# A four-stage graph network: head 3's attention weights turned by transfers, first questions by node chunk, bias rows added by transfers, terms dealt anew

## The chip, the cores and the metric

The kernel runs on one core of one Trainium2 chip. The metric is device time in microseconds, the median of several executions. TensorE does the matrix products, VectorE and ScalarE the elementwise work, and transfers are issued from the queues of SyncE (SP) and GpSimd (POOL).

## The reference, cut to what matters

512 nodes with 512 features pass through four residual stages. The first is a graph convolution. The second is a transformer of four blocks with four heads each, whose attention runs over the edges. The third is a diffusion over the graph. The fourth is a relational convolution of two layers, whose weights are sums over 30 basis matrices for each of two relations. The parts that the change touches, by their algebra:

```python
# second stage, block i; src, dst: 16384 edges among 512 nodes
y = cond_layer_norm(x, cond, s1, b1)
q = (y @ wq + bq) * 128 ** -0.5          # 4 heads of 128
k = y @ wk + bk
v = y @ wv + bv
scores = sum(q[src] * k[dst])            # per edge and head
attn = softmax of scores over the edges of each src
x = x + (segment_sum(attn * v[dst], src) @ wo + bo)
y = cond_layer_norm(x, cond, s2, b2)
x = x + relu(y @ m_w1 + m_b1) @ m_w2 + m_b2
# fourth stage, layer l
w = einsum('rb,bio->rio', att_l, basis_l)   # 2 relations, 30 bases of 512 x 512
msg = sigmoid(x_j @ gate_w[r]) * x_j @ w[r] # r by edge type
out = segment_sum(msg, row) + x @ root + bias
```

## The kernel before

The 512 nodes lie in four chunks of 128 partitions (K = 4), and so do the features. Everything is float32 except parts of the graph's counts. The edges are first turned into dense matrices of counts between nodes. Attention is therefore dense: the scores of a head are a 512 x 512 product, to which `lnC` (the logarithm of the number of edges, very negative where there is none) is added.

The order of instructions on each engine is the order in which the program writes them (`tc.manual_schedule()`), and each engine takes its queue in that order. No planner decides anything. Tiles come from pools: a tile under a name that is in use waits until the old one's readers are done. `one` has one buffer for each name, so `v`, `oT`, `mod` and `yT` are each taken in turn by several things. `weights` has four buffers of 1 MB, `rows` two, `turned` and `pT` two each, `bases` three. In PSUM, `mm` (name `ps`) has two banks, `tr` two and `sp` four.

One block `i` goes as follows.

- The first normalisation leaves `yT`, chunk by chunk. Behind each chunk's transposes (`norm_T`) TensorE computes the values of that chunk (`v_part(c)`, L832). That covers the wait for the next chunk.
- Three projections follow (`q_of`, `k_of`, L943), and then head after head: `weigh_head` computes four score chunks (L959), VectorE adds `lnC` and finds the minimum (L963), ScalarE takes the exponential (L965), VectorE the reciprocal (L952), and ScalarE scales the weights (L955).
- The product with the values (`gather`) wants the weights transposed. For heads 0 to 2, `turn_by_blocks` transposes 32 x 32 blocks on VectorE (L978), and 16 transfers from SyncE's queue put the blocks in their places (L983). For head 3, `turn` uses 16 transposes on TensorE (L121) and copies on ScalarE (L122).
- `rows_of` multiplies by `wo`, the result is added to `z` (L1077), and `norm_chunk` normalises it again under a new `mod` (`modulation`, L702 and L704).
- The MLP's first product is taken in two halves of the nodes (`m1`, L1087). The second is added to `z` (L1117) and normalised for the next block.
- The rows `bo` and `m_b2` are added to all of `z` by four VectorE instructions each (`add_row`, L992).

Beside this, VectorE computes the weights of the fourth stage. `relation_weights` is a generator: each step adds one basis times a scalar to `wrel` (L218), and is called a term below. `more(n)` puts the next n terms into VectorE's queue at that place, so where each `more` stands decides what waits behind terms. A basis is loaded from POOL's queue (L202), two ahead. There are 120 terms, and two empty steps after the last of layer 0, while `wrel` of that layer is written out to `w1d` (L220) to make room for layer 1.

The tail has the second MLP product into `x` (L1160), the diffusion (L1167, L1177, L1179) and the two relational layers.

Of the kernel before, what the change touches and what calls it, by code (L numbers as in the profile page):

```python
# [19 lines left out]
P = 128  # L20
# [47 lines left out]
def network(ctx, tc, a, out, flag_i, general):  # L68
# [17 lines left out]
    def by_partition(v):  # L86
        return v.rearrange("(k p) o -> p k o", p=P)

    def load_w(src):
        w = weights.tile([P, K, D], F32, name="w")  # L90
        nc.sync.dma_start(w, by_partition(src))
        return w
# [105 lines left out]
    def relation_weights():  # L198

        def load(l, b):  # L200
            t = pools["bases"].tile([P, K * D], F32, name="basis")
            nc.gpsimd.dma_start(t.rearrange("p (k o) -> p k o", k=K), by_partition(a[f"L3_gnn_basis{l + 1}"][b]))  # L202
            return t

        todo = [(l, b) for l in range(2) for b in range(BASES)]
        ahead = [load(*todo[i]) for i in range(2)]
        for i, (l, b) in enumerate(todo):
            if b == 0:
                wrel.append([pools["w"].tile([P, K * D], F32, name=f"wrel{r}") for r in range(R)])
            if i + 2 < len(todo):  # L210
                ahead.append(load(*todo[i + 2]))
            t = ahead[i]
            for r in range(R):
                s, w = att[:, l, r * BASES + b : r * BASES + b + 1], wrel[l][r]
                if b == 0:
                    nc.vector.tensor_scalar(w, t, s, None, op0=OP.mult)
                else:
                    nc.vector.scalar_tensor_tensor(w, t, s, w, op0=OP.mult, op1=OP.add)  # L218
                if l == 0 and b == BASES - 1:
                    nc.gpsimd.dma_start(w1d[:, r, :], w)  # L220
                yield
            if l == 0 and b == BASES - 1:

                yield
                yield

# [14 lines left out]

    def load_block(i, names):
        return [load_w(a["L1_gnn_" + n][i]) for n in names]

# [473 lines left out]
    nc.sync.dma_start(C1d, C01[:, 1, :, :])  # L718
    wv, wq, wk = load_block(0, ("wv", "wq", "wk"))

# [103 lines left out]
    def enter_d(c):  # L824
        n = rsqrt_end(*inner[c])
        nc.vector.scalar_tensor_tensor(ys[c], ys[c], n, mod[:, 1, c, :], op0=OP.mult, op1=OP.add)

    def v_part(c):
        if general:
            nc.vector.tensor_tensor(v[:, c, :], nodes(yT, c, wv), bv_row, op=OP.add)  # L830
        else:
            nc.scalar.copy(v[:, c, :], nodes(yT, c, wv))  # L832
# [63 lines left out]
    s_start(1)  # L896
    v = one.tile([P, K, D], F32, name="v")
    v_part(0)
    enter_b(2)
# [7 lines left out]
    enter_d(2)  # L907
    v_part(1)
    enter_b(3)
# [6 lines left out]
    if not general:  # L916
# [3 lines left out]
        nc.vector.tensor_scalar(flag_i, ps[:1, :1], 0.5, None, op0=OP.is_gt)  # L920
    v_part(2)
    enter_d(3)
# [15 lines left out]
    with ExitStack() as ph:  # L938
# [6 lines left out]

        def weigh_head(qT, kT):

            ps_, done = [], []

            def finish_chunk():  # L950
                c, p, st = done.pop(0)
                nc.vector.reciprocal(st[:, 2:3], st[:, 1:2])  # L952
                if general:
                    nc.vector.tensor_mul(st[:, 2:3], st[:, 2:3], has[:, c : c + 1])
                nc.scalar.mul(p, p, st[:, 2:3])  # L955

            for c in range(K):
# [7 lines left out]
                nc.scalar.activation(p, ns, AF.Exp, bias=st[:, 0:1], scale=-1.0, accum_out=st[:, 1:2])  # L965
                ps_.append(p)
                done.append((c, p, st))
                if c:
                    finish_chunk()
            finish_chunk()  # L970
            return ps_

        def turn_by_blocks(ps_):


            t = att_p.tile([P, 4, K, K, 32], F32, name="turned", bufs=2)
            for c in range(K):
                nc.vector.transpose(t[:, :, :, c, :].rearrange("p b k i -> p k b i"),  # L978
                                    ps_[c].rearrange("p (k b i) -> p k b i", k=K, b=4))
            pT = att_p.tile([P, 4, K, P], F32, name="pT", bufs=2)  # L980
            for a in range(4):
                for b in range(4):
                    nc.sync.dma_start(pT[32 * b : 32 * b + 32, a, :, :], t[32 * a : 32 * a + 32, b, :, :, :])  # L983
            return pT

        def turn(pT, ps_, cs):
            for c in cs:
                transposed(pT[:, :, chunk(c)], [ps_[c][:, chunk(k)] for k in range(K)], nc.scalar.copy)

        def add_row(row):  # L990
            for c in range(K):
                nc.vector.tensor_tensor(z[:, c, :], z[:, c, :], row, op=OP.add)  # L992

        for i in range(NB):
            oT = one.tile([P, H, N], F32, name="oT")
            turned = []

            def gather(j):


                pT, o, bias = turned[j], oT[:, j, :], bv[:, i, j : j + 1]
                bank = dict(pool=sp, name="sp") if j > 1 else {}
                if j < H - 1:
                    ps = product([(v[:, k, chunk(j)], pT[:, :, k, :]) for k in range(K)], **bank)
                    ps = ps.rearrange("p (a c i) -> p a c i", a=4, c=K)
                    o = o.rearrange("p (c a i) -> p a c i", c=K, a=4)
                else:
                    ps = product([(v[:, k, chunk(j)], pT[:, k, :]) for k in range(K)], **bank)
                if general:
                    nc.vector.tensor_copy(o, ps)  # L1010
                else:
                    nc.scalar.activation(o, ps, AF.Identity, bias=bias)

# [6 lines left out]

            q, k = [q_of(0)], [k_of(0)]
            q.append(q_of(1))
            for j in range(H):
                head = weigh_head(q[j], k[j])
                if j < H - 1:
                    turned.append(turn_by_blocks(head))
                if j == 0:
                    k.append(k_of(1))
                    q.append(q_of(2))
                    more(1)  # L1030
                elif j == 1:
                    k.append(k_of(2))
                    v_part(3)
                    more(2)
                elif j == 2:
                    gather(0)
                    mod = new_mod()
                    modulation(mod, 0)
                    q.append(q_of(3))
                    k.append(k_of(3))  # L1040
                    gather(1)
                    add_row(bo)
                    more(3)
            w1, w2 = load_block(i, ("m_w1", "m_w2"))
            b2 = load_row(a["L1_gnn_m_b2"][i])

# [7 lines left out]

            ps_ = [rows_of(c, (0, 1)) for c in range(2)]
            more(6)
            pT = att_p.tile([P, K, N], F32, name="pT", bufs=2)
            turn(pT, head, range(K))
            turned.append(pT)
            modulation(mod, 1)  # L1060
            if i < NB - 1:
                modulation_loads(i + 1, 1)
            if i == 0 and not general:
                missed = nc.values_load(flag_i[:1, :1], min_val=0, max_val=1)
            gather(3)
            gather(2)
            yT = one.tile([P, K, N], F32, name="yT")
            ys = []
            for c in range(K):
                if c < 2:  # L1070
                    ps = rows_of(c, (3, 2), ps_[c], last=True)
                else:
                    ps = rows_of(c, (0, 1))
                    if c == 3:
                        norm_T(yT, ys[1], 1)
                    rows_of(c, (2, 3), ps, last=True)
                nc.vector.tensor_tensor(z[:, c, :], ps, z[:, c, :], op=OP.add)  # L1077
                ys.append(norm_chunk(mod, c))
                if c == 2:
                    norm_T(yT, ys[0], 0)  # L1080
            tT = one.tile([P, K, N], F32, name="oT")

# [13 lines left out]
            m1(0, 3)  # L1096
            add_row(b2)
            if i == NB - 1:
                for c in range(K):
                    nc.vector.tensor_tensor(x[:, c, :], z[:, c, :], x[:, c, :], op=OP.add)  # L1100
            else:
                wv, wq, wk, wo = load_block(i + 1, ("wv", "wq", "wk", "wo"))
                if general:
# [17 lines left out]
            norm_T(yT, ys[1], 1)  # L1121
            v = one.tile([P, K, D], F32, name="v")
            v_part(0)
            more(1)
            norm_T(yT, ys[2], 2)
            v_part(1)
            more(1)
            norm_T(yT, ys[3], 3)
            v_part(2)
            more(7)  # L1130
# [35 lines left out]
    for c in range(K):  # L1166
# [4 lines left out]
        if c:  # L1171
            more(1)
    hT = one.tile([P, K, N], F32, name="yT")
# [136 lines left out]
```

## Time and profile before

| | |
|---|---|
| time, median of 3 runs (lowest to highest) | 833.35 us (833.02 to 836.57) |
| the profiled execution: its own time | 833.25 us |
| its span | 831.5 us |
| TensorE busy (PE) | 807.9 us, 97% |
| VectorE busy (DVE) | 678.5 us, 82% |
| ScalarE busy (ACT) | 325.2 us, 39% |
| terms (L218), 116 of them | 264.9 us on VectorE, 2343 ns each |
| granted TensorE clock | 0.999 |

The span is the time from the first to the last instruction that was profiled. The execution's own time is 1.75 us longer. In a timeline a line gives the start in the span, the duration, the engine and line of the code, what is written and read, and how many instructions were merged; in brackets stands the idle time before it and what ended that. Records of f32 matrix products come in pairs, two for a call. Busy time of TensorE is no measure of its work, since the end of each product is modelled and products overlap.

### The profile page before, as it was taken

The page shows a single profiled execution, that of the slowest core. Times are in us where ns is not written, and L with a number is a line of the kernel's source. Part 1 is how long each engine was busy: PE and PEld are TensorE (multiplying, and loading weights), DVE is VectorE, ACT ScalarE, POOL GpSimd, SP SyncE. Part 2 cuts the span into 40 slices and gives each one's busy share as a digit, 9 for nine tenths or more (in the row PEclk, how much of TensorE's full clock was granted, in tenths as well). Part 3 has the DMA queues.
Part 4 walks back from the last instruction along what each step waited for, and adds up shares of the span by engine and source line. Part 5 has one row for each costly group of instructions (what it writes and reads, how often), then busy time and mean ns, then how long its engine had stood idle before and what let it go on. Part 6 is the DMA issues. An engine that isn't in the chain of part 4 may idle for free.

```text
span 831.5 us, 8251 instructions
## 1 busy us (share of the span) xinstructions
PE 807.9 (97%) x2597; PEld 392.6 (47%) x2597; DVE 678.5 (82%) x1199; ACT 325.2 (39%) x657; POOL 64.4 (8%) x135
## 2 busy tenths in 40 slices
PE   7999999999999999999999999999999999999997
PEld 4444344454444644445644445544445544444445
DVE  5977986978899999799997889998899977787530
ACT  5454414544662424652324652325653122310410
POOL 8000010000000101010101010110010100010000
PEclk9999999999999999999999999999999999999999
DMA  9200164305677646588547585655599721231001
GB/s 228 75 7 17 43 221 184 114 1 165 187 233 253 207 139 202 149 256 276 177 153 269 149 268 201 203 177 172 147 310 362 227 71 53 76 103 50 1 13 40
DMA packets 50833, 128.38 MB, mean 154 GB/s; under 512 B 7008, under 2 KB 7808, under 8 KB 49760
## 3 DMA queue, kind: packets, MB, share of 16 engines
q0 software_dynamic: 17552, 66.83, 25.5%
q1 hardware_dynamic: 32944, 60.84, 23.2%
q8 instruction: 22, 0.36, 0.2%
q14 instruction: 27, 0.22, 0.1%
q10 hardware_dynamic: 288, 0.13, 0.1%
HBM read 108.90 MB, written 6.29 MB: 139 GB/s over the span
## 4 chain that ended last, share of the span: by engine, by line
PE 56%; DVE 27%; ACT 6%; issue 4%; SPq 4%; DMA 2%; DVEq 0%; ACTq 0%
PE ps L101 28%; DVE wrel L218 13%; PE sp L101 6%; PE ps L1087 5%; PE win L598 5%; PE ps L376 5%; SPq L983 3%; ACT p L965 2%; PE sp L959 2%; DVE st L158 2%; PE tr L121 2%; DVE turned L978 2%; PE sp L702 1%; DMA pT<-turned 1%; DVE z L992 1%
## 5 line engine op out<-in xcount | busy, mean ns | idle before, releaser
L218 DVE SCALAR_TENSOR_TENSOR wrel<-basis,att,wrel 128x2048 f32<-128x2048 f32 x116 | 264.9, 2343 | 0.0
L101 PE MATMUL ps<-w,oT 128*128 128x512 f32 (+1 forms) x296 | 129.7, 584 | 1.0 <-DVE x L1160 1.0
L101 PE MATMUL ps<-yT,w 128*128 128x512 f32 x256 | 112.9, 594 | 0.0
L101 PE MATMUL ps<-w,yT 128*128 128x512 f32 x224 | 101.1, 595 | 1.2 <-ACT yT L128 0.7
L202 POOL DMA_DIRECT2D basis<-in_L_gnn_basis_dram x60 | 45.1, 752 | 676.0 <-DVE wrel L218 517.1
L101 PEld LDWEIGHTS ps<-w,oT 128*128 128x128 f32 x296 | 54.6, 190 | 63.9 <-issue 55.2
L101 PEld LDWEIGHTS ps<-yT,w 128*128 128x128 f32 x256 | 48.2, 190 | 61.9 <-issue 61.2
L101 PEld LDWEIGHTS ps<-w,yT 128*128 128x128 f32 x224 | 41.1, 190 | 47.7 <-issue 44.7
L1087 PE MATMUL ps<-yT,w 128*128 128x256 f32 x256 | 58.5, 382 | 2.9 <-ACT yT L122 2.9
L133 ACT ACTIVATE g<-mv,eps_t 128x1 f32<-128x1 f32 (+1 forms) x45 | 13.2, 294 | 121.2 <-DVE mv L160 120.1
L965 ACT ACTIVATE p<-ns,stat 128x512 f32<-128x512 f32 x64 | 45.5, 711 | 31.1 <-DVE stat L963 30.9
L959 PE MATMUL sp<-kT,qT 128*128 128x512 f32 x128 | 57.5, 592 | 0.0
L1087 PEld LDWEIGHTS ps<-yT,w 128*128 128x128 f32 x256 | 47.4, 190 | 14.3 <-ACT yT L122 6.2
L598 PE MATMUL win<-s_hot,st 128*128 128x512 bf16 x195 | 51.2, 381 | 0.0
L963 DVE CUSTOM_DVE_ANT_0 ns<-sp,lnC 128x512 f32<-128x512 f32 x64 | 43.2, 689 | 5.5 <-PE sp L959 5.5
L579 DVE TENSOR_SCALAR s_hot<-node_ids,e_c 128x512 bf16<-128x512 f16 x128 | 39.6, 355 | 6.1 <-PE win L598 5.9
L955 ACT ACTIVATE p<-p,stat 128x512 f32<-128x512 f32 x64 | 43.7, 706 | 0.0
L959 PEld LDWEIGHTS sp<-kT,qT 128*128 128x128 f32 x128 | 24.3, 190 | 30.6 <-issue 30.1
L704 ACT ACTIVATE mod<-sp 128x512 f32<-128x512 f32 x64 | 32.9, 599 | 8.6 <-PE sp L702 8.6
L598 PEld LDWEIGHTS <-st 128*128 128x128 bf16 x195 | 18.6, 98 | 37.3 <-issue 24.1
L952 DVE RECIPROCAL stat<-stat 128x1 f32<-128x1 f32 x64 | 10.4, 163 | 29.8 <-ACT p L965 29.6
L121 PEld LDWEIGHTS tr<-ident,y 128*128 128x128 f32 x176 | 21.5, 141 | 20.7 <-issue 19.4
(273 smaller groups left out, 1097.7 us busy)
## 6 DMA issues: line engine op xcount, KB each, us to landing
basis<-in_L_gnn_basis_dram POOLq DMA_DIRECT2D x60, 1024.0 KB, 6.8
pT<-turned SPq DMA_DIRECT2D x192, 64.0 KB
w<-in_L_gnn_m_w_dram SPq DMA_DIRECT2D x8, 1024.0 KB
w<-in_L_gnn_wv_dram SPq DMA_DIRECT2D x4, 1024.0 KB
w<-in_L_gnn_wq_dram SPq DMA_DIRECT2D x4, 1024.0 KB
w<-in_L_gnn_wk_dram SPq DMA_DIRECT2D x4, 1024.0 KB
w<-in_L_gnn_wo_dram SPq DMA_DIRECT2D x4, 1024.0 KB
w1d<-wrel POOLq DMA_DIRECT2D x2, 1024.0 KB, 6.2
```

The costliest lines, as they stand in the source:

```text
L101: nc.tensor.matmul(ps, lhsT, rhs, start=(first and i == 0), stop=(last and i == len(parts) - 1))
L121: nc.tensor.transpose(ps[:, i, :], b, ident)
L202: nc.gpsimd.dma_start(t.rearrange("p (k o) -> p k o", k=K), by_partition(a[f"L3_gnn_basis{l + 1}"][b]))
L218: nc.vector.scalar_tensor_tensor(w, t, s, w, op0=OP.mult, op1=OP.add)
L376: nc.tensor.matmul(bank[0], lhsT, rhs, start=(i == 0), stop=(i == len(parts) - 1))
L579: nc.vector.tensor_scalar(s, node_ids, src[:, c : c + 1], None, op0=OP.is_equal)
L598: nc.tensor.matmul(banks[w], st[:, c - g0, :, :], s, start=(left[w] == total[w]), stop=(left[w] == 1))
L955: nc.scalar.mul(p, p, st[:, 2:3])
L959: nc.tensor.matmul(ps, qT[:, chunk(c)], kT, start=True, stop=True)
L963: nc.vector.tensor_tensor_reduce(ns, ps, lnC[:, c, :], -1.0, 3e38, OP.add, OP.min, st[:, 0:1])
L965: nc.scalar.activation(p, ns, AF.Exp, bias=st[:, 0:1], scale=-1.0, accum_out=st[:, 1:2])
L1087: nc.tensor.matmul(ps[:, :256], w1[:, k, chunk(j)], yT[:, k, cols], start=(k == 0), stop=(k == K - 1))
```

## The change

- All heads are turned by blocks. `weigh_head` now transposes the blocks itself, chunk 0 ahead of the last chunk's reciprocal. `bring` issues the 16 transfers. Heads 0 and 1 are brought into a `mod` tile that is free at that time, heads 2 and 3 into `pT`.
- The questions and keys of heads 0 and 1 are computed by node chunk behind `norm_T` (`qk_part`, 128 columns a call), where the values were computed. The values follow during heads 2 and 3 and behind them. `qk` and `v` share a buffer.
- The rows `bo` and `m_b2` are added by accumulating transfers from POOL's queue. In the last block `m_b2` is added to `x` at the block's start.
- Terms: none between the heads, 11 after head 3, 6 and 9 later in the block; in the diffusion two in place of one behind each chunk. At the meeting of the layers the last two bases of layer 0 and the first two of layer 1 are taken relation by relation, and the two empty steps are gone. A basis is loaded when one has been used up, three at the start.
- Weights are loaded in the order wq, wk, wv, wo.
- In the second normalisation, chunk 2's `norm_chunk` is written behind the transposes of chunk 1.

```diff
@@ relation_weights
-        ahead = [load(*todo[i]) for i in range(2)]
+        order = [(l, b, r) for l in range(2) for b in range(BASES) for r in range(R)]
+        meet = slice(2 * BASES - 4, 2 * BASES + 4)
+        order[meet] = [(l, b, r) for l, bs in ((0, (BASES - 2, BASES - 1)), (1, (0, 1))) for r in (1, 0) for b in bs]
+        bases = {i: load(*i) for i in todo[:3]}
...
+            used[l, b] += 1
+            if used[l, b] == R and len(bases) < len(todo):
+                i = todo[len(bases)]
+                bases[i] = load(*i)
+            yield
...
+    def qk_part(i, c):
+        ps = mm.tile([P, D], F32, name="ps")
+        for n, (w, j) in enumerate(((wk, 0), (wq, 0), (wk, 1), (wq, 1))):
+            calls(ps[:, chunk(n)], [(w[:, k, chunk(j)], yT[:, k, chunk(c)]) for k in range(K)])
+        for n, b in enumerate((bk, bq, bk, bq)):
+            nc.scalar.activation(qk[:, n, chunk(c)], ps[:, chunk(n)], AF.Identity,
+                                 bias=b[:, i, n // 2 : n // 2 + 1], scale=qscale if n % 2 else 1.0)
...
@@ weigh_head
+            t = att_p.tile([P, 4, K, K, 32], F32, name="turned", bufs=2)
...
+            turn_blocks(0)
             finish_chunk()
-            return ps_
+            for c in range(1, K):
+                turn_blocks(c)
+            if j < 2:
+                if j == 0:
+                    spare.append(new_mod())
+                pT = spare[0][:, j, :, :].rearrange("p a (k n) -> p a k n", k=K)
+            else:
+                pT = att_p.tile([P, 4, K, P], F32, name="pT", bufs=2)
+            return t, pT
...
-        def turn(pT, ps_, cs):
-            for c in cs:
-                transposed(pT[:, :, chunk(c)], [ps_[c][:, chunk(k)] for k in range(K)], nc.scalar.copy)
-        def add_row(row):
-            for c in range(K):
-                nc.vector.tensor_tensor(z[:, c, :], z[:, c, :], row, op=OP.add)
+        def add_row(t, row):
+            nc.gpsimd.dma_start(t, row.unsqueeze(1).to_broadcast([P, K, D]), accum_op=OP.add)
...
@@ a block
-            q, k = [q_of(0)], [k_of(0)]
-            q.append(q_of(1))
+            add_row(z, bo)
+            if i == NB - 1:
+                add_row(x, load_row(a["L1_gnn_m_b2"][i]))
+            qk_part(i, 3)
+            k, q = [qk[:, 0, :], qk[:, 2, :]], [qk[:, 1, :], qk[:, 3, :]]
+            q.append(q_of(2))
             for j in range(H):
-                head = weigh_head(q[j], k[j])
...
+                weighed = weigh_head(j, q[j], k[j])
+                if j == 2:
+                    v = one.tile([P, K, D], F32, name="v")
+                    v_part(0)
+                elif j == 3:
+                    v_part(1)
+                turned.append(bring(*weighed))
                 if j == 0:
-                    k.append(k_of(1))
-                    q.append(q_of(2))
-                    more(1)
+                    k.append(k_of(2))
                 elif j == 1:
...
+            v_part(2)
+            v_part(3)
...
-            ps_ = [rows_of(c, (0, 1)) for c in range(2)]
-            more(6)
-            pT = att_p.tile([P, K, N], F32, name="pT", bufs=2)
-            turn(pT, head, range(K))
-            turned.append(pT)
+            more(11)
+            gather(0)
+            gather(1)
+            mod = new_mod()
+            modulation(mod, 0)
+            ps_ = [rows_of(0, (0, 1))]
             modulation(mod, 1)
+            ps_.append(rows_of(1, (0, 1)))
...
+            gather(2)
             gather(3)
-            gather(2)
...
-            add_row(b2)
...
+                add_row(z, b2)
...
@@ next block's first chunks
-            v = one.tile([P, K, D], F32, name="v")
-            v_part(0)
+            qk = one.tile([P, 4, N], F32, name="v")
+            qk_part(i + 1, 0)
             more(1)
...
@@ diffusion
         if c:
-            more(1)
+            more(2)
```

## The prediction

> **What bounds the kernel now.** I read the page's engine totals, then one attention block (block 1) queue by queue in the timelines, then the tail. All times are microseconds from the start of the span.
>
> ```profile
> span 831.5 us, 8251 instructions
> PE 807.9 (97%) x2597; PEld 392.6 (47%) x2597; DVE 678.5 (82%) x1199; ACT 325.2 (39%) x657; POOL 64.4 (8%) x135
> ```
>
> TensorE looks like the bound, but its timeline shows few holes and VectorE's shows almost none either. VectorE in block 1, from the score minimum of head 0 (call it D) to the first `z` addition behind the attention (call it Z):
>
> ```profile
> 302.35 20.44 DVE L218 SCALAR_TENSOR_TENSOR wrel<-basis,att,wrel 128x2048 f32<-128x2048 f32 x9
> 322.72 0.68 DVE L963 CUSTOM_DVE_ANT_0 ns<-sp,lnC 128x512 f32<-128x512 f32 x1
> ...
> 330.34 2.31 DVE L218 SCALAR_TENSOR_TENSOR wrel<-basis,att,wrel 128x2048 f32<-128x2048 f32 x1
> 332.57 0.68 DVE L963 CUSTOM_DVE_ANT_0 ns<-sp,lnC 128x512 f32<-128x512 f32 x1
> ...
> 337.79 2.49 DVE L978 STREAM_TRANSPOSE turned<-p 128x512 f32<-128x512 f32 x4
> 340.20 4.57 DVE L218 SCALAR_TENSOR_TENSOR wrel<-basis,att,wrel 128x2048 f32<-128x2048 f32 x2
> ...
> 352.40 2.46 DVE L992 TENSOR_TENSOR z<-z,row 128x512 f32<-128x512 f32 x4
> 354.77 6.87 DVE L218 SCALAR_TENSOR_TENSOR wrel<-basis,att,wrel 128x2048 f32<-128x2048 f32 x3
> ...
> 366.55 13.64 DVE L218 SCALAR_TENSOR_TENSOR wrel<-basis,att,wrel 128x2048 f32<-128x2048 f32 x6
> 380.13 0.69 DVE L1077 TENSOR_TENSOR z<-ps,z 128x512 f32<-128x512 f32 x1
> ```
>
> VectorE has no long wait between 322.72 and 380.13: four heads, four row additions, twelve terms, end to end. TensorE has its output rows for the 380.13 addition ready at about 379.9. So both engines bound the block at once, and work taken from one alone buys nothing. TensorE around the turn of head 3 and the start of the MLP:
>
> ```profile
> 366.46 1.04 PE L121 MATMUL tr<-ident,p 128*128 128x128 f32 x8
> 368.19 1.14 PE L121 MATMUL tr<-ident,p 128*128 128x128 f32 x8 [0.69 <-ACT pT L122]
> ...
> 390.45 1.99 PE L1087 MATMUL ps<-yT,w 128*128 128x256 f32 x8 [0.72 <-ACT yT L122]
> ```
>
> The third queue is SyncE's:
>
> ```profile
> 330.45 32.10 SPq L983 DMA_DIRECT2D pT<-turned  x48
> ```
>
> Forty-eight transfers in 32.1, 0.63 to 0.64 each where no wait shows, 10.1 a head. It has no room to spare once a fourth head is added.
>
> **The change, part by part.**
>
> *Head 3 by blocks.* Removed per block: 16 transposes, 0.109 each start to start (four in 0.435), 1.7, and the hole of 0.69. Added: four block transposes on VectorE (2.49 for four) and 16 transfers on SyncE (10.1).
>
> *Questions by chunk.* q0, k0, q1, k1 become 64 calls of 128 columns. The trace has such calls once:
>
> ```profile
> 185.95 1.06 PE L101 MATMUL sp<-CP,AT 128*128 128x128 f32 x8
> ```
>
> Eight records (two a call), next start 0.89 later: 0.111 a record against 0.43 for 512 columns, so a chunk costs 32 x 0.111 = 3.55 against 3.44: +0.1, and 1.8 over 16 chunks. The Trainium skill speaks against the edit here: "TensorE: Matmul & The Clock Gate", section Back-to-back issue gap, puts a sustained stream of weight load and 128-column matmul at about 81 ns instead of the isolated 56. A bf16 call of 512 columns takes 0.216 here, so an f32 record is two passes and the row is 56 ns a pass; at 81 the chunk would cost 5.2, and 16 of them +28. I take the row; it is the same form, though only eight records long.
> ScalarE gets four 128-column evacuations a chunk, about 0.36 each (extrapolated from 0.47 for 256 columns and 0.69 for 512), under 3.5 of matmuls.
> The values move behind the scores, where TensorE used to have questions and keys. Their copies sit on ScalarE behind head 3's exponentials, which I count below.
>
> *D to Z, after.* With no term between heads the pitch of a head on VectorE is 5.1 to its last reciprocal, and three block transposes of 0.62 (the first now fits in the 1.15 wait before that reciprocal): 7.1. Head 0's transfers start at D+7.1, head 1's follow on SyncE, ending at D+7.1+20.3 = D+27.4. `turned` has two buffers, so head 3's first block transpose, natural at about D+25, waits for head 1's last transfer to land: the packets in the trace trail an issue by 1 to 1.5, and gather(0) at 344.59 bounds it by 3.4, so D+28.9. Then 2.7 (four transposes and a reciprocal) and 11 terms of 2.27: Z = D+56.6. TensorE: scores, k2, q3, k3 and values; the last value chunk waits for a PSUM bank that ScalarE frees only behind head 3 (about D+31), then 3.4 values, 6.9 gathers 0 and 1, 5.6 modulation and first rows, gather 2 3.4: D+50.4. Head 3's transfers end at D+27.4+20.3 = D+47.7 and land about D+49 to 52; gather 3 and the rows of chunk 0 take 5.3: Z no earlier than D+55.8 to 57.5. I take D+57.0, against 57.4 in blocks 1 and 3 and 56.9 in block 0 (199.89 to 256.82). So all that VectorE saves (2.4 of row addition, one term, 2.5 of hidden transposes) is given back as a wait for the transfers.
>
> *Z to the next stage.* The copies of yT chunks 0 and 1 no longer stand behind chunk 2's ScalarE work: y1 is ready at Z+7.05, and the MLP starts at Z+9.2 (0.44 transposes and 1.72 rows behind it) instead of Z+10.3: -1.1. The second row addition (2.49) leaves VectorE where it idled 1.18 anyway, so the rest of it is worth nothing, and TensorE sets this stretch at 30.2 instead of 31.3.
>
> *Accumulating transfers.* No such transfer is in the trace. bo has 57 of time. b2 starts when `z` is last read (Z+13) and must land by Z+30: 16 to 17. POOL's queue holds the basis loads in front, all released by then. Below: 1 MB plain, a basis load's 5.4 to 5.9; above: 3 MB of traffic with contention, three such, 17. I take 9, hidden, cost 0; if the cover goes, every microsecond past 16 counts three times. The skill's "SBUF — State Buffer", section SBUF: two separate sides, warns that GpSimd-issued transfers stall while VectorE runs two-port operations. That would push it, and the basis loads, past the cover. Basis loads issued in the middle of terms landed in 5.8 here, so I don't count it.
>
> *Terms dealt anew.* 26 a block, 11 in one run. With three buffers a load has 9.1 to land; loads beside weight loads landed in 8.6 to 9.2 in block 1. No charge, but no slack. At the meeting of the layers the empty slots are gone: block 2 gets one more real term ahead of D (+2.3, of which TensorE's own lateness there had covered some), and inside the run of 11 `wrel` waits for the write of w1 (6.2 to land, two terms of 4.55 between, +0.7 issue): +2.5. Block 2's Z was 503.01, set by TensorE; now 443.85+2.27+57.0+2.5 = 505.6: +2.6 instead of -0.4.
>
> *Tail.* Block 3 loses one row addition ahead of the `x` sums: VectorE, late there (TensorE waits 1.02 at 659.50), is 2.4 earlier. But the diffusion gets two terms per chunk:
>
> ```profile
> 676.45 2.34 DVE L218 SCALAR_TENSOR_TENSOR wrel<-basis,att,wrel 128x2048 f32<-128x2048 f32 x1
> 679.71 0.69 DVE L1167 TENSOR_TENSOR mod<-ps,row 128x512 f32<-128x512 f32 x1 [0.92 <-PE ps L101]
> 680.32 2.34 DVE L218 SCALAR_TENSOR_TENSOR wrel<-basis,att,wrel 128x2048 f32<-128x2048 f32 x1
> 683.14 0.69 DVE L1167 TENSOR_TENSOR mod<-ps,row 128x512 f32<-128x512 f32 x1 [0.48 <-PE ps L101]
> 683.75 2.34 DVE L218 SCALAR_TENSOR_TENSOR wrel<-basis,att,wrel 128x2048 f32<-128x2048 f32 x1
> 686.65 0.75 DVE L1177 SCALAR_TENSOR_TENSOR mod<-ps,rinv,mod 128x512 f32<-128x512 f32 x1 [0.55 <-PE ps L101]
> ```
>
> Three more terms, 6.8, against holes of 0.92+0.48+0.55: +4.8 at 686.65. From there normalisation, gates and message products follow VectorE, so it stays.
>
> *Sum* against the profiled execution's 833.25 (span 831.5; median 833.35): Z +0.1 in block 0, -0.4 in blocks 1 and 3, +2.6 in block 2; three times -1.1; tail -2.4+4.8: +1.0. For head 3's transfers meeting basis loads (below) I add 0.2 a block: 835.
>
> **Rivals.**
> *Transfers starve (slower).* While a basis load moves, SyncE's queue nearly stops: in the packets of 223 to 227 and 344 to 348 it moves under 45 KB a microsecond, else 100 and more. Now a load leaves every 4.6 just while heads 2 and 3 are carried, and in the program's order each SyncE transfer waits for the eighth before it. Head 3 landing at D+54 instead of 51 makes Z D+59.4, +2.4 in four blocks: 845; at D+56, 853. Against it: the backlog was caught up within 2 each time.
> *Accumulation late (slower).* Landing 20 after issue, 4 to 6 past the cover, three times: 850. It decides from 16.
> *VectorE's saving comes through (faster).* If the first transfers, free of loads, run at the shortest seen (0.51 instead of 0.63), Z moves to D+54 in four blocks, -3 each, and TensorE's 1.2 fewer a block come through: 823 to 826. Against it: 0.63 holds also in 336 to 343, without loads.
> That nothing happens is no case: each queue is rewritten.
>
> **How the numbers follow.** About 0.5% (4.2) is what a measurement can tell. As laid out 0.50 (829 to 841, centre 835), starving 0.22 (840 to 853), late accumulation 0.12, faster 0.16 (822 to 829). Faster 0.17, same 0.42, slower 0.41. The range for 8 in 10 reaches from the edge of the faster case into starving: 826 to 850.
>
> **What would show it.** Right: VectorE idle 2 to 4 before head 3's first block transpose, released by a transfer; SyncE's transfers one run of about 40; D to Z near 57; MLP start at Z+9.2; the S products about 1.4 late at chunk 0. Wrong: TensorE idle before gather 3 or the second `z` addition, terms waiting for a basis load, 128-column calls above 0.12 a record, an accumulating transfer above 16.

## The result, and the profile after

| | before | after |
|---|---|---|
| median of 4 runs (lowest to highest) | 833.59 us (833.02 to 836.57) | 872.41 us (869.68 to 876.95) |
| ratio, 95% interval | | 1.0464 (1.0406 to 1.0521) |
| profiled execution: own time, span | 833.25, 831.5 | 876.95, 875.2 |

The change made the kernel 38.8 us slower; 835.0 with a range of 826 to 850 was predicted. The profiled execution of after is the longest of its four runs, 4.5 above their median, so sums over its trace come out a little large. From its page:

```profile
span 875.2 us, 9047 instructions
PE 820.9 (94%) x2917; PEld 424.9 (49%) x2917; DVE 668.5 (76%) x1183; ACT 324.0 (37%) x689; POOL 75.6 (9%) x143
PEclk9999999999999999989999989999898999999999
PE 48%; DVE 20%; SPq 12%; DMA 11%; ACT 5%; issue 5%; DVEq 0%; ACTq 0%
```

VectorE is busy 10 us less, as the change set out to do, yet the span is 44 longer. The granted clock, 9 in all slices before, dips in four. The last line is the chain of waits: SyncE's queue and the transfers hold 23% of it, where they held 6% before.

The two traces are compared by the prediction's marks: D (head 0's first score minimum) and Z (the first `z` addition behind the attention).

| stretch | before | after | sum of the differences |
|---|---|---|---|
| D to Z, four blocks | 56.9, 57.4, 58.1, 57.4 | 64.3, 65.5, 68.7, 70.6 | +39.2 |
| Z to second z addition, three blocks | 31.3 each | 30.3 each | -3.0 |
| second z addition to next D | 34.6, 33.5, 34.6 | 34.6, 34.9, 34.6 | +1.4 |
| last Z to the x sums | 32.4 | 30.0 | -2.4 |
| x sums to the S products | 27.9 | 32.5 | +4.6 |
| start to the first D; S products to the end | 199.9; 144.8 | 202.1; 146.5 | +2.2; +1.7 |

D to Z holds 39.2 of the 43.7 by which the two spans differ; the other rows come to 4.5 in sum. The list of waits, with the sum, the number and the longest of each, names the places:

```profile
PE sp L101 <- DMA pT<-turned: 21.4, 4, 6.7
PE ps L101 <- ACT v L845: 13.5, 4, 5.5
DVE turned L974 <- DMA mod<-turned: 28.2, 9, 5.5
DVE z L1093 <- PE ps L101: 30.2, 4, 9.1
```

TensorE waits in every block for head 3's transfers (first line) and for ScalarE at the last value chunk (second). VectorE waits at `turned` for heads 0 and 1, and at Z for TensorE. Block 1, with the start and the duration in front: SyncE, then VectorE, then TensorE.

```profile
338.15 20.44 SPq L1005 DMA_DIRECT2D mod<-turned  x32
358.69 23.11 SPq L1005 DMA_DIRECT2D pT<-turned  x32
...
360.11 0.71 DVE L974 STREAM_TRANSPOSE turned<-p 128x512 f32<-128x512 f32 x1 [3.92 <-DMA mod<-turned]
362.58 20.44 DVE L222 SCALAR_TENSOR_TENSOR wrel<-basis,att,wrel 128x2048 f32<-128x2048 f32 x9
396.78 0.69 DVE L1093 TENSOR_TENSOR z<-ps,z 128x512 f32<-128x512 f32 x1 [7.93 <-PE ps L101]
...
362.15 3.70 PE L101 MATMUL ps<-w,yT 128*128 128x512 f32 x8 [1.44 <-ACT v L845]
378.79 3.60 PE L101 MATMUL sp<-pT,v 128*128 128x512 f32 x8
388.81 6.03 PE L101 MATMUL sp<-pT,v 128*128 128x512 f32 x8 [6.42 <-DMA pT<-turned]
```

SyncE issues heads 0 and 1 at 0.639 a transfer, heads 2 and 3 at 0.722. Its last issue ends at 381.8, and gather 3 is released at 388.81, 7 later. That is D+57.6, where the prediction had head 3 land by D+52; in blocks 0, 2 and 3 it is D+57.0, D+61.5 and D+62.3. Gather 3 then takes 6.03, where the same eight records of gather 2 took 3.60. Why the queue is slow shows in the transfer view of 367 to 370. The run of terms has released its first basis load at 365.19, and the next three follow at 369.71, 374.24 and 378.76. The view gives packets, MB and the share of the engines' time:

```profile
q0 software_dynamic: 201, 0.82, 81.6%
q1 hardware_dynamic: 15, 0.03, 2.6%
```

q0 carries the basis loads, q1 SyncE's transfers. SyncE issued four transfers of 64 KB here (367.50, 368.13, 368.82, 369.40), and 0.03 MB moved. From 370.0 on its issues stall as well, since each waits for the eighth before it to land: behind that of 370.0 the next starts 1.65 later, behind that of 376.2 2.39 later, instead of 0.63. With no load beside it the queue moves the 100 KB a microsecond that SyncE issues. What has piled up it moves faster: in before, 0.46 MB from 348 to 350, when a single load was nearly through.

### The profile page after: what moved, and what is told of

It is laid out like the page before. It is cut to its first block, busy times and chain, and to the rows that moved or that the text cites. A ratio compares the mean times of both kernels' runs of the same rounds, so it can differ in the third digit from the quotient of the medians.

```text
span 875.2 us, 9047 instructions
## 1 busy us (share of the span) xinstructions
PE 820.9 (94%) x2917; PEld 424.9 (49%) x2917; DVE 668.5 (76%) x1183; ACT 324.0 (37%) x689; POOL 75.6 (9%) x143
## 4 chain that ended last, share of the span: by engine, by line
PE 48%; DVE 20%; SPq 12%; DMA 11%; ACT 5%; issue 5%; DVEq 0%; ACTq 0%
PE ps L101 22%; SPq L1005 11%; DVE wrel L222 10%; DMA pT<-turned 9%; PE sp L101 8%; PE ps L1104 5%; PE win L602 5%; PE ps L380 5%; ACT p L985 3%; PE tr L121 2%; DVE st L158 1%; DMA w<-in_L_gnn_W_mlp_dram 1%; DVE turned L974 1%; ACT p L971 1%; PE sp L706 1%
## 5 line engine op out<-in xcount | busy, mean ns | idle before, releaser
L101 PE MATMUL ps<-w,yT 128*128 128x512 f32 x224 | 106.4, 624 | 14.1 <-ACT v L845 13.5
L101 PE MATMUL ps<-yT,w 128*128 128x128 f32 (+1 forms) x640 | 115.7, 339 | 0.5 <-ACT yT L122 0.5
L101 PEld LDWEIGHTS ps<-yT,w 128*128 128x128 f32 x640 | 82.0, 192 | 29.9 <-issue 29.2
L101 PEld LDWEIGHTS ps<-w,yT 128*128 128x128 f32 x224 | 43.9, 200 | 70.5 <-issue 50.3
L974 DVE STREAM_TRANSPOSE turned<-p 128x512 f32<-128x512 f32 x64 | 41.1, 685 | 29.2 <-DMA mod<-turned 28.2
L101 PE MATMUL sp<-pT,v 128*128 128x512 f32 x64 | 37.4, 739 | 21.4 <-DMA pT<-turned 21.4
L1104 PEld LDWEIGHTS ps<-yT,w 128*128 128x128 f32 x256 | 47.4, 190 | 10.6 <-ACT oT L1106 3.1
L101 PE MATMUL ps<-mod,v 128*128 128x512 f32 x96 | 42.8, 595 | 1.8 <-DVE mod L1184 1.1
L101 PEld LDWEIGHTS sp<-pT,v 128*128 128x128 f32 x64 | 14.9, 240 | 42.9 <-issue 41.9
## 6 DMA issues: line engine op xcount, KB each, us to landing
z<-row POOLq DMA_DIRECT2D x7, 1024.0 KB, 10.5
```

The source lines that it names most:

```text
L101: nc.tensor.matmul(ps, lhsT, rhs, start=(first and i == 0), stop=(last and i == len(parts) - 1))
L1104: nc.tensor.matmul(ps[:, :256], w1[:, k, chunk(j)], yT[:, k, cols], start=(k == 0), stop=(k == K - 1))
```

## The experiments

Each ratio is to before, measured beside the run (medians of 833.6 to 834.4). The theory: *starving*. The run of eleven terms releases a basis load every 4.5 us while heads 2 and 3 are carried, and the small transfers hardly move beside it. Rivals: 64 transfers in a row are too slow by themselves; w1 and w2, queued behind head 3, take the bandwidth; ScalarE holds the value chunks; questions by chunk, row transfers or the dealing of terms cost by themselves. In what follows, "wait" without more is TensorE's wait for head 3 ahead of gather 3, and "value wait" that for ScalarE at the last value chunk.

**1. No basis loads.**

```diff
-                bases[i] = load(*i)
+                bases[i] = bases[todo[len(bases) % 3]]
```

> The changed kernel with all basis loads but the first three left out (the terms read those three again), so the relation weights are not the reference's. Starving (my theory: a basis load leaves every 4.6 us beside the run of eleven terms and nearly stops SyncE's small transfers): heads 2 and 3 are issued at 0.63 to 0.64 a transfer instead of 0.72, head 3 lands within 2 of its last issue, the wait of TensorE ahead of gather 3 (3.8 to 6.7) falls under 2, gather 3 takes 3.5 instead of 5.4 to 6.3, D to Z is 57 to 59 instead of 64 to 71, the total 840 to 848. Serial issue alone (64 transfers in a row on one queue are too many, loads or not): the wait stays at 3 or more and the total is above 860. Weight loads (w1 and w2, which follow head 3 on the same queue, take its bandwidth): same, above 860. Value copies (ScalarE holds TensorE at the last value chunk): waits of 1.4 to 5.5 at the value chunk stay, D to Z 61 and more.

Measured: 834.59, ratio to before 1.0006 (0.9992 to 1.0020), better than the expected 840 to 848. D to Z 59.1, 56.4, 58.5, 56.6, and no wait for head 3 at all. SyncE issues heads 2 and 3 at 0.63 to 0.69 over the blocks, against 0.70 to 0.81 in after. The transfer view of SyncE's two heads in block 1 (352 to 373.6):

```profile
q1 hardware_dynamic: 1530, 2.09, 39.5%
```

2.09 MB in 21.6 us are 97 KB a microsecond. In after, the same two heads (358.7 to 381.8) shared the time:

```profile
q0 software_dynamic: 826, 3.20, 45.1%
q1 hardware_dynamic: 1409, 1.92, 33.0%
```

So 64 transfers in a row are fast enough, and leaving the basis loads out removes 37.8 of the 38.8. That is more than head 3's part alone: the row transfers, which stand behind loads in POOL's queue, also left earlier (183.1 instead of 200.9 in block 0). Runs 4, 8 and 9 take those apart. Before was not run without its loads; with them its D to Z, 57.5 on average, is already that of this run, 57.6. Value waits of 1.3 to 3.2 stayed, as that rival said, but without its price.

**2. Head 3 on TensorE again.** `weigh_head` turns no blocks for head 3, `turn`'s 16 transposes stand ahead of gather 2; all else as changed.

> The changed kernel with head 3 alone turned by TensorE as before, all else as changed. Starving: with 48 transfers instead of 64, most of them issued before the run of terms begins, nothing on the path waits for a transfer: D to Z 56.5 to 58.5, the total 829 to 836 (872.4 less four times 7.4 to 13.2). Value copies: the last value chunk still waits for head 3's exponentials, but VectorE's wait of 3.9 ahead of head 3 is gone with its block transposes, so it shrinks under 1. If the cost lies in the chunked questions, the accumulating transfers or the dealing of terms: above 855.

Measured: 843.56, ratio 1.0094 (1.0067 to 1.0120), above the expected 829 to 836. 29 of the loss are gone, not all: D to Z 56.2, 57.1, 63.7, 60.2. In block 3 there was a value wait of 2.8. In block 2, where terms also waited 3.46 for the write of w1 and 3.20 for a basis, head 2's transfers (issued from 471.8 to 488.1) were late in their turn:

```profile
494.48 9.97 PE L101 MATMUL sp<-pT,v 128*128 128x512 f32 x16 [3.51 <-DMA pT<-turned]
```

Neither questions by chunk nor row transfers cost 20 by themselves. But head 2 starves too where traffic meets it: here the write of w1 (472.9) and three basis loads (473.9, 481.2, 483.6). Which of the four did it was not taken apart.

**3. Half of the rows ahead of gather 3.**

```diff
             gather(2)
+            ps_ += [rows_of(c, (0, 1), pool=sp, name="sp") for c in (2, 3)]
             gather(3)
...
-                    ps = rows_of(c, (0, 1))
+                    ps = ps_[c]
```

> The changed kernel with the first half of the output rows of chunks 2 and 3 (heads 0 and 1, eight records, 3.5 us) moved ahead of gather 3, into two free PSUM banks, so that TensorE works where it waited. Clock (my theory for the part that the wait itself does not explain: the granted clock falls after TensorE's idle 4 to 7 us, so that gather 3 takes 5.4 to 6.3 instead of 3.5 and the rows behind it are slow too): gather 3 takes 3.5 to 3.8, its landing wait shrinks by 3.5, D to Z falls by 2 to 3 a block, and Z to the start of the MLP by up to 1 since the rows of chunks 2 and 3 are half done; total 856 to 864. If the slow records come from something else than idleness (memory traffic, data): gather 3 stays at 5.4 or more, D to Z stays, and the total falls by under 4.

Measured: 874.63, ratio 1.0458 (1.0418 to 1.0499); the total missed the expected 856 to 864. D to Z fell (62.9, 62.3, 67.6, 70.2), but Z to the MLP grew from 9.4 to 10.8, since VectorE's additions and normalisations now set the pace there (TensorE waits 2.85 for chunk 1's `y` in block 1). Gather 3 took 3.67 in blocks 0 and 1 (idle before it: none and 2.02) and 5.37 in blocks 2 and 3 (2.79 and 1.99). So slow records were part of the loss, and filling the wait removed them in two blocks. Run 13 takes up why.

**4. Before, with row transfers and chunk 2 normalised later.**

> The kernel before with two parts of the change alone: the bias rows added by accumulating transfers, and chunk 2 normalised after the copies of chunks 0 and 1 (heads, questions, terms and tail as before). By the steps that the trace after bore out: Z to second z addition 30.3 instead of 31.3 in three blocks, about as much at the fourth block's MLP, 2.4 less ahead of the x sums, D to Z unchanged since TensorE bounds it too: total 825 to 828. If the row additions by VectorE had been on the path of D to Z: down to 818. If an accumulating transfer holds z or x past its reader beside the old order of loads: 833 or more.

Measured: 838.74, ratio 1.0050 (1.0032 to 1.0067): 11 above the expected 825 to 828. D to Z is 59.0, 57.2, 64.7 and 64.9. In block 2 `z`'s row transfer leaves POOL at 443.68, and it and the basis load behind it land at 456 and 461. In block 3 `z`'s leaves at 570.45 and x's at 571.23; x's and the basis load behind it land at 588 and 592. Head 0's sixteen transfers are issued in that time, from 451.9 to 465.8 and from 581.5 to 596.1. In block 1 the row transfer (319.5) and the load (323.3) landed at 330 and 333, while head 0 began at 330.7, and nothing was lost. TensorE at gather 0 in block 3:

```profile
601.48 5.61 PE L101 MATMUL ps<-pT,v 128*128 128x512 f32 x8 [5.89 <-DMA pT<-turned]
```

The same starving, from another source. (The 2.0 of block 0 are something else: terms wait there for a late basis load, and so they do in run 9, which has no row transfer.)

**5. The same, row transfers behind head 2's terms.**

> The kernel before with the same two parts as in the run that added bias rows by transfers and normalised chunk 2 later (838.7), but with the bo and x row transfers issued behind head 2's three terms instead of at the block's start. If those transfers cost because they move beside head 0's small transfers (starving again, from another source: in blocks 2 and 3 head 0 landed 4.7 late): D to Z back to 57 to 58 in blocks 2 and 3 (64.7 and 65.1 there), total 824 to 829. If the loss there comes from the b2 transfers in the MLP or from the order of normalising: still above 835.

Measured: 852.75, ratio 1.0222 (1.0205 to 1.0239), far above the expected 824 to 829. Part of the forecast held: D to Z 58.1, 57.2 and 60.2 in blocks 0 to 2 (64.7 in block 2 before the move). Block 3 took 77.3. x's row is loaded by SyncE, behind 48 transfers; x's transfer waited for it in POOL's queue, and two basis loads stood behind. POOL, then VectorE:

```profile
618.02 1.30 POOL L991 DMA_DIRECT2D x<-row  x1 [14.65 <-DMA row<-in_L_gnn_m_b_dram]
618.79 2.11 POOL L202 DMA_DIRECT2D basis<-in_L_gnn_basis_dram  x2
...
641.56 4.61 DVE L218 SCALAR_TENSOR_TENSOR wrel<-basis,att,wrel 128x2048 f32<-128x2048 f32 x2 [20.35 <-DMA basis<-in_L_gnn_basis_dram]
```

Those loads landed 23 to 26 after their issue. A transfer's place in the program is a place in two queues: that of its own engine, and that of the transfer it waits for.

**6. A candidate: head 3 on TensorE, terms 1, 2, 3 and 6 as before, row transfers behind head 2, one term a chunk in the diffusion.**

> A candidate: the changed kernel with head 3 on TensorE, the terms dealt as before in a block (1, 2, 3 behind heads 0 to 2, 6 behind head 3), the bo and x row transfers behind head 2's terms, and one term a chunk in the diffusion. Starving: no wait for a transfer on TensorE, D to Z 56 to 57.5, Z to second z addition 30.3, x sums to S product 27.9 as before, total 820 to 828. If the questions by chunk or the values behind the scores cost by themselves: 833 or more. If the terms between the heads now hold VectorE at the layers' meeting: 826 to 832.

Measured: 881.88, ratio 1.0576 (1.0555 to 1.0597), the worst of all. The value placement does cost, once terms stand between the heads:

```profile
375.87 6.37 PE L101 MATMUL ps<-w,yT 128*128 128x512 f32 x8 [8.55 <-ACT v L845]
```

The copy that frees the bank is queued on ScalarE behind head 3's exponentials, and those wait for VectorE, which six terms delay. Over four blocks: 34.7. So the change's parts hang together. Values behind the scores need heads without terms between them, that puts eleven terms behind head 3, and those release the loads that starve its transfers. One expectation held: with one term a chunk in the diffusion the x sums stand 27.92 ahead of the S products, as before, where two terms give 32.48.

**7. w1 and w2 loaded later, by ScalarE behind gather 2.**

> The changed kernel with w1 and w2 (2 MB) not loaded by SyncE right behind head 3's transfers but by ScalarE behind gather 2. Starving by basis loads alone: head 3 lands at most 2 earlier, total 864 to 874. Weight loads take the bandwidth of head 3's last transfers: the landing trails the last issue by 2 to 3 instead of 7, D to Z falls by 4 to 6 in each block, total 850 to 858. Either may be blurred if the weights come late for the MLP (Z to the MLP's start above 9.4).

Measured: 871.41, ratio 1.0443 (1.0426 to 1.0461). The weight loads left behind the start of gather 3 in blocks 0 to 2, and the wait in the four blocks is 3.1, 6.2, 6.5, 2.9, against 3.8, 6.4, 6.7, 4.5. So the weight loads are not the cause.

**8. bo on VectorE behind the eleven terms, and the last b2 on VectorE in the MLP, as in before.**

> The changed kernel with bo (and the last block's b2 for x) added by VectorE again, behind the run of eleven terms, where it idles 7.9; the three b2 additions stay transfers. If the bo and x transfers starve heads 0 and 1 (which then hold `turned`, VectorE, ScalarE and the last value chunk: waits of 2.9, 1.4, 3.6, 5.5): the value wait falls to 1.3 to 2 in all blocks and its slow records go, D to Z 62 to 65 in all four instead of 64.3, 65.5, 68.7, 70.6, total 860 to 866 (2.4 of it given back by the additions for x). If they do no harm: 872 to 877.

Measured: 870.32, ratio 1.0444 (1.0418 to 1.0470), so the total hardly moved and lies between the two forecasts. The value waits did fall, from 13.5 to 6.3 in sum, and block 3 from 70.6 to 65.0. So the bo and x transfers do starve heads 0 and 1. But a TensorE that comes earlier waits longer for head 3, 24.6 in sum instead of 21.4:

```profile
PE sp L101 <- DMA pT<-turned: 24.6, 4, 8.0
PE ps L101 <- ACT v L845: 6.3, 4, 2.1
```

**9. Before, with chunk 2 normalised later, and nothing else.**

```diff
                     norm_T(yT, ys[1], 1)
+                    ys.append(norm_chunk(mod, 2))
                 rows_of(c, (2, 3), ps, last=True)
...
-                ys.append(norm_chunk(mod, c))
                 if c == 2:
                     norm_T(yT, ys[0], 0)
+                else:
+                    ys.append(norm_chunk(mod, c))
```

> The kernel before with one part of the change alone: chunk 2 normalised, and its ScalarE work issued, only after the transposes of chunk 1. The trace after showed the MLP start at Z+9.4 instead of Z+10.3 and Z to second z addition 30.3 instead of 31.3; if that comes from this order alone: 830.0 to 831.0 (three blocks at 1.0; the last block is held by VectorE's row addition there). If it needed the row additions by transfers as well: 833 to 834.

Measured: 831.51, ratio 0.9971 (0.9961 to 0.9982). The MLP starts at Z+9.43 and the second `z` addition comes at Z+30.3: this order alone makes the gain. Against run 4, which differs by the row transfers alone, those cost 7.2 net of what they take off VectorE.

**10. The same, and the last b2 onto x by a transfer in block 1's MLP.** A candidate.

> The same, and besides only one bias row as a transfer: the last block's b2 goes onto x in block 1's MLP, 200 us before it is needed and where no small transfer is near; all else of the bias rows stays on VectorE. If transfers do no harm where no small transfer moves: 1.5 to 2.4 less than the run with the order of normalising alone (Z to the x sums 30.0 instead of 32.4 in the last block), 827.5 to 829. If an accumulating transfer costs wherever it lies (a late basis load): no better than 831.

Measured: 828.36, ratio 0.9930 (0.9918 to 0.9942): faster than both kernels. The transfer took 14.8 to land, with no head's transfer in flight; Z to the x sums is 30.0. (D to Z is 60.6 in block 2 of the profiled execution, the slowest of six, since a term waits 2.73 for a basis load there, 78 us after the transfer has landed.)

**11. Every second basis load left out.**

> The changed kernel with every second basis load left out (the terms read the basis before once more), so that behind head 3 a load leaves every 9.1 us instead of every 4.6; the relation weights are not the reference's. Starving as a matter of the loads' rate: D to Z between 57.6 (no loads) and 67.3 (all), near 61 to 63, gather 3's wait 1 to 3, total 845 to 860. If it were a threshold (a queue that only two loads in flight starve): under 842. If the loads' number did not matter but their mere presence: above 864.

Measured: 850.03 (846.09 to 851.99), ratio 1.0187 (1.0159 to 1.0215). D to Z 60.3, 60.4, 66.5, 57.7, on average 61.2, between 57.6 without loads and 67.3 with all. So the loss grows with the rate of the loads.

**12. A second candidate: head 3 on TensorE, eleven terms in one run, bo on VectorE behind them, x's row as in run 10, one term a chunk in the diffusion.**

> A second candidate: the changed kernel with head 3 on TensorE (843.6 so), bo added by VectorE behind the run of eleven terms, the last b2 onto x by a transfer in block 1's MLP, and one term a chunk in the diffusion. Taking the run with head 3 on TensorE: minus 4.6 for the diffusion, minus 2.5 to 3.5 in the last block (60.2 to 57), minus 0 to 3 in block 2, where the transfers no longer meet w1's write: 831 to 837. If the eleven terms and the row additions together make VectorE the bound: 838 or more. If it were as good as its best block (56.2) in all: 826.

Measured: 829.28, ratio 0.9937 (0.9924 to 0.9950), better than the expected 831 to 837: D to Z 56.2, 57.1, 58.4, 57.1, with no value wait, and one wait of 1.3 ahead of gather 2 in block 2 as the only one for a transfer. With 48 small transfers a block and no row transfer near them, the path hardly waits for a transfer any more. Its interval overlaps that of run 10, and no run tells the two apart.

**13. A product of eight records, result not read, between gather 2 and gather 3.**

> The changed kernel with one product of eight records more (3.4 us, result not read) between gather 2 and gather 3, where TensorE waits 3.8 to 6.7 for head 3. If the slow records of gather 3 (5.3 to 6.3) come from the idle time before them: with under 3.4 of idle left, gather 3 takes 3.5 to 3.7 in all four blocks, D to Z falls by 1.7 to 2.7 a block, total 862 to 867. If the traffic that moves then slows the records (1.03 of the DMA engines' time busy): gather 3 stays at 5.3 or more and the total at 870 to 875. If the filler itself stands in the way: more than 875.

Measured: 867.23, ratio 1.0386 (1.0357 to 1.0415). Gather 3 took 3.67 in blocks 0 and 3, where 0.9 and 0.4 of idle time were left, and 5.37 and 5.36 in blocks 1 and 2, where it was 2.55 and 5.44. Stretches of gather 3 in blocks 0 and 1 (start, end and length, busy times and counts of PE, PEld, DVE, ACT and POOL, then granted clock, share of the DMA engines, GB/s):

```profile
258.20:262.00 3.80, 3.72 (x9) 1.82 (x10) 0.25 (x1) 0.01 (x1) 0.75 (x1) 1.00 1.04 390
385.80:391.30 5.50, 5.41 (x9) 2.41 (x10) 0.00 (x0) 0.00 (x0) 0.75 (x1) 0.69 1.04 388
```

The DMA engines are as busy in both. The clock differs, and so does the idle time before. The tail of after has the reverse case, eight records behind an idle time of 2.69 with no transfer moving at all:

```profile
740.30:745.70 5.40, 5.40 (x9) 2.38 (x10) 4.69 (x12) 1.07 (x3) 0.00 (x0) 0.68 0.00 0
```

They are just as slow. So the records are slow from idling, not from traffic.

## Why the prediction was wrong, point by point

- **The step that failed** is the landing of head 3: "Head 3's transfers end at D+47.7 and land about D+49 to 52". In block 1 the last issue ended at D+50.6 and the landing came at D+57.6. The allowance for meeting basis loads, 0.2 a block, was the mis-sized term: D to Z takes 67.3 on average with all loads and 57.6 without them, so it measures 9.6 a block. The wait ahead of gather 3 was 3.8 to 6.7 with all loads, none without them (run 1), and 1.2 to 3.4 with half of them (run 11). The mechanism stood among the rivals, as transfers that starve, with a chance of 0.22 and 853 as its worst.
- **Why it was set aside:** "the backlog was caught up within 2 each time". That was read from single loads, and read rightly (0.46 MB from 348 to 350). Loads that leave every 4.5 and land in 7 to 10 overlap, and leave no gap in which to catch up. The interval stood in the same paragraph.
- **A second price was missing.** After a wait of some length the clock falls: gather 3 took 5.4, 6.0, 5.3 and 6.3 instead of 3.6, 8.6 in sum, and three of the four last value chunks 5.2 to 6.3 instead of 3.7. The prediction counted a late transfer as its wait alone. The tail pays this price too: with two terms a chunk TensorE waits 2.69 for ScalarE's copy behind the S products, instead of 0.58, and the eight records that follow take 5.40. In runs 8 and 11, with the same wait, they took 3.70, and the stretch to the end 144.8 to 144.9 as in before. That is the +1.7.
- **The accumulating transfers** landed as estimated (median 10.5, estimated 9), and those that had to land within 16 took 8.1 to 9.7, so the rival that they land late is dead. That they are "hidden, cost 0" was wrong: what they cost is the delay of the small transfers beside them. Run 4 against run 9 prices it at 7.2; in after most of it hid behind head 3 (run 8).
- **The value chunk** was to wait for ScalarE "to about D+31": D+30.9 in block 1, but D+32.8 and D+35.0 in blocks 2 and 3, since heads 0 and 1 landed late there. The wait comes down to 1.1 to 2.2 in run 8 and to nothing in run 12.
- **Right, by the traces:** head 3 on VectorE done at D+31.3 (predicted 31.6), with its wait of 3.9 (2 to 4). D to Z without loads 57.6 on average (57.0), so the rest of that sum stands. The start of the MLP at Z+9.4 (9.2), the row addition off the tail -2.4 (-2.4), the diffusion +4.6 (+4.8). A chunk of questions, 32 records, takes 3.57 from start to start, 0.111 a record: the row of eight held over a sustained stream, and the 81 ns that the Trainium skill, "TensorE: Matmul & The Clock Gate", section Back-to-back issue gap, puts on one did not: with two passes a record, 0.111 is 56 ns a pass. Terms waited 2.6 for the write of w1 (+2.5). They also waited for bases, a sign named for being wrong, up to 1.5 and 5.8 in sum, but VectorE was done with them 6 to 9 before Z in every block, so this cost nothing.
- **VectorE's saving** did not come through as a rival of its own. Run 12 shows what it is worth with the transfers out of the way: D to Z 57.2 on average, against 57.5 before. Most of that run's gain comes from Z and the tail.
- **Left open:** the +2.2 before the first D, which is about the spread between kernels with the same code there (199.1 to 201.2). Loads gated to keep clear of head 3, with all heads turned by blocks, were not tried.

## What to carry to other kernels

A load that is released by computing leaves when that computing runs. Moving instructions in one queue therefore moves transfers in another, and what has to be asked is which small transfer on the path is in flight then. Price a late transfer with the clock it costs afterwards, not with the wait alone. Taking work off an engine is worth nothing while the path waits for a queue: runs 10 and 12 keep only what hardly touches the busy queues, and gain 0.6 to 0.7%.

## What the runs showed of the hardware

- Beside GpSimd's loads SyncE's small transfers got little. In the three microseconds shown, the DMA engines moved 201 packets of 4 KB for the first and 15 of 2 KB for the second, with four transfers issued on SyncE in that time. From 366 to 382 SyncE's queue got 1.15 of 4.40 MB, where it moves 1.6 in 16 us with no load beside it. The Trainium skill, "DMA: Bandwidth & Descriptors", section Queues, rings and completion order, has each DMA engine go round its queues packet by packet. Over the 16 us the trace would agree, 838 packets to 842, but 281 of the second are of 4 bytes and 45 of the first, and whether the profile's packets are the page's is not shown. Within a few microseconds it disagrees, and those decide how long SyncE waits for the eighth transfer before. What decides the order there was not tested.
- TensorE's clock fell after shorter waits than the skill's "TensorE: Matmul & The Clock Gate", section Part 1, puts it, about 3.4 us of idleness. Eight records took 5.37 to 5.40 after 1.97 (run 1), 1.99 (run 3), 2.15 (run 8) and 2.55 us (run 13), and 3.67 to 3.70 after 2.02 (run 3), 2.75 (run 13) and 2.83 (run 2). After 2.69 in the tail they took 5.4 or more in after and five runs, and 3.70 in two. Of all products of eight such records behind one wait of 1.5 us or more, none was slow up to 1.84, some were and some were not between 1.97 and 2.83, and all were from 2.88 on. Run 9 has one more, 5.40 behind two short waits of 1.24 and 0.46 at 165.
- A product of eight records behind such a fall took 5.1 to 6.8 instead of 3.6, so it cost 1.5 to 3.2 more.
